# Layer 2 spectra of a four-layer kernel: three samples' image norms stepped behind the stages of the next sample's 7x7 windows, and two samples' transforms interleaved

## The chip, the cores and the metric

The kernel runs on one core of a Trainium2 chip. The metric is the device time of one execution in microseconds. All data and arithmetic of the parts discussed here are float32.

## The reference, cut to what matters

The input is `x`, (4, 56, 56, 128). Four layers follow each other, each with a group norm in front and a residual around it: a 7x7 window attention with a global attention and an MLP (layer 0), an edge network (layer 1), a Fourier-operator attention over images (layer 2), and a temporal convolution (layer 3). Only the entry of layer 2 is touched.

```python
x = x + _L2_conv_ref(_gn(x), ...)          # _gn: group norm, 32 groups of 4 channels
# inside layer 2; B, T, H, W = 4, 56, 56, 128 (a 56 x 128 image per row of the tensor)
xa = x.reshape(B * T, 1, H, W)
xa_n = _inorm(xa, norm_g[0], norm_b[0])    # mean and variance of each whole image
k = _fno_layer(xa_n, wK, wKs, bKs, (H // 2, W // 2))   # each begins with rfft2(xa_n)
q = _fno_layer(xa_n, wQ, wQs, bQs, (H // 2, W // 2))
v = _fno_layer(xa_n, wV, wVs, bVs, (H, W))
```

So before any spectrum can be formed, a sample needs its group norm (mean and variance of 4 channels over all pixels) and its 56 image norms (mean and variance of 56 x 128 values each). The kernel calls the group-normed sample `xad`. It needs it again later, as the residual of layer 2.

## The kernel before, in words

A sample lies in SBUF as 128 partitions (channels) by 3136 pixels. Layers 0 and 1 run sample by sample, in `first_layers`: `fast_windows` (7x7 window attention, layer norm and the projections for the global attention), the rest of `fast_attention` (global attention), `mlp`, `edge_layer`. Their result is the tile `x1`, which is stored to DRAM as `x2d[b]` (L2424). A value that is computed at run time chooses between this fast path and a general one (`tc.If`); the fast path is the one that runs, and behind the branch all engines go on in the code for layers 2 and 3.

`fast_windows` takes a sample's 64 windows in 8 groups of 8. It is a software pipeline with 10 stages (norm, project, score, value, turn, output, central, variance, attended, divide), written out in Python loops over `n` and over the stages: at each `n` stage s works on group n minus that stage's lag. The order of TensorE (PE), VectorE (DVE) and ScalarE (ACT) is exactly the order of the Python code (`manual_schedule`). Three PSUM banks tagged `mm` rotate among the stages. After groups 3 and 7, `variance` takes a square root on ACT (L434) and a reciprocal of 128x392 on DVE (L435), which `divide` needs. Matrix products for global attention start only when the last group has left the pipeline.

Layer 2 begins in `spectra`, once all four samples are done. `normed_images` makes a sample's norms: 56 `bn_stats` (L1209), an aggregate (L1213), two small products on PE with `g4` for the group mean and variance (L1215, L1231), a square root (L1233), the scaling of the whole sample in place (`apply_norm`, L192), the store to `xad` (L1237), and two more small products for the image means and variances (L1243, L1249) with a square root and a reciprocal. `sample_spectra` makes a sample's transforms: 224 small products over the image width (L1271), scaled into `z` by DVE (L1273) and copied by ACT (L1275), then the products over the height (L1281, L1293 with ACT copies, and L1303 with copies shared by DVE and ACT). Both are generators. The last sample is still in SBUF (`x1`) and goes first: all its norms, then its transforms; the norms of the next sample are stepped between the pieces of the transforms, and whatever is left of them runs before the next transform begins. The other three samples are loaded back from `x2d` (L1203).

SyncE (SP) issues nearly all DMAs, in an order which the framework's scheduler chooses and which then is fixed. GpSimd (POOL) prepares the weights of the spectral layers (`all_score_weights`, `value_weights`) at the same time as the spectra.

Of the kernel before, what the change touches and what calls it, by code (L numbers as in the profile page):

```python
# [18 lines left out]
P = 128  # L19
# [279 lines left out]

def both_attentions(k, w, xw, xf):  # L300
    window_attention(k, w, xw, xf)
    global_attention(k, w, xf)


def fast_windows(k, w, xw, xf, mr, Q, K, V):

# [15 lines left out]
    with ExitStack() as es:  # L322
# [103 lines left out]
        def variance(g):  # L426
            q = g % HALF
            if q == 0:
                roots[g // HALF] = psum.tile([P, 512], F32, tag="var", name="w_var", bufs=1)
            var = roots[g // HALF]  # L430
            nc.tensor.matmul(var[32 * q:32 * q + 32, :N], k.ones_c[:, 0:32], squares.pop(g), start=True, stop=True)
            if q == HALF - 1:
                r = wk.tile([P, N], F32, name="w_r")
                nc.scalar.activation(r, var[:, :N], AF.Sqrt, scale=1024.0, bias=eps)  # L434
                nc.vector.reciprocal(r, r)  # L435
                roots[g // HALF] = r
# [9 lines left out]
        def attended(g):  # L446
# [7 lines left out]
            while chunk < 25 and (g == NG - 1 or chunk * P + 4 * P <= b.stop):  # L454
# [8 lines left out]
                chunk += m  # L463

        norm(0)
        norm(1)
        for n in range(NG + 11):
            for stage, g in ((norm, n + 2), (project, n), (score, n - 1), (value, n - 2), (turn, n - 3), (output, n - 4),
                             (central, n - 5), (variance, n - 6), (attended, n - 11), (divide, n - 10)):
                if 0 <= g < NG:  # L470
                    stage(g)


# [85 lines left out]

def fast_attention(k, w, xw, xf, mr):  # L560

# [8 lines left out]
    with ExitStack() as es:  # L570
# [3 lines left out]
        va = big.tile([P, 25, P], F32, name="f_va")  # L574
        fast_windows(k, w, xw, xf, mr, qT, kT, va)

# [610 lines left out]

def normed_images(k, w, st, b, pools, x2d, xad, ready):

    nc = k.nc
    wk, psum = pools

    def tiny(name):
        return wk.tile([P, HH], F32, name="s_" + name)

    if st.last == b:
        xp = st.x1
    else:  # L1200
        xp = wk.tile([P, HH + 1, HH], F32, name="s_x2")
        for t in range(0, HH, 28):
            nc.sync.dma_start(xp[:, t:t + 28, :], x2d[b, :, t:t + 28, :])  # L1203
        yield
    nc.vector.memset(xp[:, HH, :], 0.0)
    x = xp[:, :HH, :]
    rows = wk.tile([P, HH, 6], F32, name="s_rows")
    for t in range(HH):
        nc.vector.bn_stats(rows[:, t, :], x[:, t, :])  # L1209
        if t % 8 == 7:  # L1210
            yield
    mv = wk.tile([P, 2], F32, name="s_mv")
    nc.vector.bn_aggr(mv, rows.rearrange("p a b -> p (a b)"))  # L1213
    ps = psum.tile([P, 512], F32, tag="t", name="s_pt")
    nc.tensor.matmul(ps[:, 0:1], k.g4, mv[:, 0:1], start=True, stop=True)  # L1215

    half = [rows[:, :, i] for i in range(6)]
    mean, sq, d = tiny("mean"), tiny("sq"), tiny("d")
    nc.vector.tensor_sub(d, half[1], half[4])
    nc.vector.tensor_mul(d, d, d)  # L1220
    nc.vector.tensor_add(sq, half[2], half[5])
    nc.vector.scalar_tensor_tensor(sq, d, HH / 4, sq, ALU.mult, ALU.add)
    nc.vector.tensor_add(mean, half[1], half[4])
    yield
    mr = wk.tile([P, 2], F32, name="s_mr")
    t1 = wk.tile([P, 1], F32, name="s_t1")
    nc.vector.tensor_copy(mr[:, 0:1], ps[:, 0:1])
    nc.vector.tensor_sub(t1, mv[:, 0:1], mr[:, 0:1])
    nc.vector.tensor_mul(t1, t1, t1)
    nc.vector.tensor_add(t1, t1, mv[:, 1:2])  # L1230
    nc.tensor.matmul(ps[:, 1:2], k.g4, t1, start=True, stop=True)  # L1231
    yield
    nc.scalar.activation(t1, ps[:, 1:2], AF.Sqrt, bias=k.eps)  # L1233
    yield
    nc.vector.reciprocal(mr[:, 1:2], t1)
    apply_norm(k, x, x, mr)
    nc.sync.dma_start(xad[b], x)  # L1237
    ready[b] = xp
    yield
    nc.vector.tensor_scalar(mean, mean, 0.5, mr[:, 0:1], ALU.mult, ALU.subtract)  # L1240
    nc.vector.tensor_scalar_mul(mean, mean, mr[:, 1:2])
    nc.vector.tensor_scalar(sq, sq, mr[:, 1:2], mr[:, 1:2], ALU.mult, ALU.mult)
    nc.tensor.matmul(ps[:, 64:64 + HH], k.ones_c, mean, start=True, stop=True)  # L1243
    yield
    nc.vector.tensor_copy(st.norm[:, b, 0, :], ps[:, 64:64 + HH])
    nc.vector.tensor_sub(d, mean, st.norm[:, b, 0, :])
    nc.vector.tensor_mul(d, d, d)
    nc.vector.scalar_tensor_tensor(sq, d, float(HH), sq, ALU.mult, ALU.add)
    nc.tensor.matmul(ps[:, 128:128 + HH], k.ones_px, sq, start=True, stop=True)  # L1249
    yield  # L1250
    nc.scalar.activation(d, ps[:, 128:128 + HH], AF.Sqrt, bias=k.eps)
    yield
    nc.vector.reciprocal(d, d)
    nc.vector.tensor_scalar_mul(st.norm[:, b, 1, :], d, w.ng[:, 0:1])
    yield


def sample_spectra(k, st, b, pools, x):

    nc = k.nc
    wk, psum = pools

    z = wk.tile([P, 33, 2 * HH], F32, name="s_z")
    xf = x.rearrange("p t h -> p (t h)")
    for t0 in range(0, HH, 14):
        ps = psum.tile([P, 512], F32, tag="row", name="s_pr")
        for t in range(14):
            for ri in range(2):  # L1270
                nc.tensor.matmul(ps[64 * ri:64 * ri + 64, t * 33:(t + 1) * 33],  # L1271
                                 xf[:, (t0 + t) * HH:(t0 + t) * HH + 64], k.fw[:, ri, :], start=True, stop=True)
        nc.vector.tensor_mul(z[:, :, t0:t0 + 14], ps[:, :462].rearrange("p (t f) -> p f t", t=14),  # L1273
                             bc(st.norm[:, b, 1, t0:t0 + 14], 1, 33))
        nc.scalar.copy(z[:, :, HH + t0:HH + t0 + 14], z[:, :, t0:t0 + 14])  # L1275
        yield
    o = slice(64 * (b % 2), 64 * (b % 2) + 64)
    for c0, c1, v in C_BLOCKS_S:
        ps = psum.tile([P, 512], F32, tag="acc", name="s_ps")
        m = (c1 - c0) * HH  # L1280
# [8 lines left out]
    for blocks in (C_BLOCKS_R[:2], C_BLOCKS_R[2:]):  # L1289
        ps = psum.tile([P, 512], F32, tag="acc", name="s_pr2")  # L1290
        for i, (c0, c1, v) in enumerate(blocks):
# [8 lines left out]
    for c0 in range(0, 32, 4):  # L1300
        ps = psum.tile([P, 512], F32, tag="acc", name="s_px")
        for i in range(4):
# [5 lines left out]

def spectra(k, w, st, x2d, xad):

# [3 lines left out]
    for t in (st.S, st.iS, st.R):  # L1314
        nc.gpsimd.memset(t[:, :, :, HH:], 0.0)
    ready = {}
    with ExitStack() as es:
# [4 lines left out]
                                                     mybir.EngineType.DVE}))  # L1322

        order = [st.last] + [b for b in range(B) if b != st.last]
        norms = [normed_images(k, w, st, b, (wk, tiny), x2d, xad, ready) for b in order] + [iter(())]
        next(norms[1])
        for _ in norms[0]:
            pass
        for n, b in enumerate(order):
            ahead = norms[n + 1]  # L1330
            for _ in sample_spectra(k, st, b, (wk, psum), ready.pop(b)):
                next(ahead, None)
            for _ in ahead:
                pass

# [1032 lines left out]
def build(k, packs, I, out):  # L2368
# [3 lines left out]
    with ExitStack() as es:  # L2372
# [10 lines left out]

        l2p = es.enter_context(tc.tile_pool(name="l2", bufs=1))
        with tc.tile_pool(name="w01", bufs=1) as wp, tc.tile_pool(name="io", bufs=1) as io:
            xw = io.tile([P, TOK], F32, name="xw")
# [29 lines left out]
            def first_layers(attention, x, to, loaded=False):  # L2416
# [6 lines left out]
                edge_layer(k, w1, x1, st)  # L2423
                nc.sync.dma_start(to, x1)  # L2424

            with tc.If(small_scores > 0) as small:
                for b in range(B):
                    first_layers(lambda *a: fast_attention(*a, k.mr[:, b, :]), I["x"][b], x2d[b],
                                 loaded=b == 0)
            with small.Else():  # L2430
                with tc.For_i(0, B, 1) as b:
                    first_layers(both_attentions, I["x"][bass.ds(b, 1)].rearrange("b p t -> (b p) t"),
                                 x2d[bass.ds(b, 1)].rearrange("b p l n -> (b p) l n"))

        l3p = es.enter_context(tc.tile_pool(name="l3", bufs=1))
        load_weights(k, l3p, I, "w3_", w2)
        load_weights(k, l3p, I, "w2_", w2, only=CONV_WEIGHTS)
        st = Env()
        st.x1, st.last = x1w, B - 1
        st.norm = l3p.tile([P, B, 2, HH], F32, name="norm")  # L2440
        st.AbT = l3p.tile([P, 2, HH], F32, name="AbT")
        st.dc = l3p.tile([1, B, HH], F32, name="dc")
        with tc.tile_pool(name="xh", bufs=1) as xp:
            st.xh = xp.tile([112, B, 2, 32, HH], F32, name="xh")
            with tc.tile_pool(name="sp", bufs=1) as sp:
# [4 lines left out]
                with tc.tile_pool(name="g_wk", bufs=1, side="right") as wk:  # L2450
                    all_score_weights(k, I, w2, sp, wk, st)
                    value_weights(k, I, w2, wk, dd)
                    spectra(k, w2, st, x2d, xad)
                x1s.close()
# [32 lines left out]
```

## Time and profile before

| | us |
|---|---|
| median of 3 runs (lowest to highest) | 3901.99 (3901.64 to 3906.46) |
| profiled execution, its own time | 3907.5 |
| its span, first to last instruction | 3905.7 |
| `fast_windows` of samples 0, 1, 2, 3, to the first product of the global attention | 53.8 to 155.5, 759.9 to 860.1, 1463.4 to 1563.1, 2168.7 to 2269.0 |
| last instruction of the last edge layer (DVE L966) | 2869.2 to 2869.9 |
| spectra: first `bn_stats` (L1209) to last copy into `xh` (ACT L229) | 2872.2 to 2913.0 for the first of the four samples, to 3013.4 for all |

The mean granted TensorE clock of the execution is 0.954. Of the span PE is busy 91%, DVE 74%, ACT 53%, POOL 30%.

Times in the profile are microseconds from the start of the span, unless ns is written. A line number is that of the kernel before. A row of a timeline or of the chain has start, duration, engine, line, operation or tile, and a count; square brackets hold the idle time of the engine before the row and what ended it. A table of windows has, for each stretch, its length and the busy time and instruction count of PE, PEld (weight loads), DVE, ACT and POOL, then the granted clock and the DMA share and rate.

### The profile page before, as it was taken

To read this page: it belongs to the slowest core of one execution; us is meant where nothing else is said; L and a number is where in the kernel's file an instruction comes from. 1 tells how busy PE (TensorE), PEld (TensorE's weight loads), DVE (VectorE), ACT (ScalarE), POOL (GpSimd) and SP (SyncE) were. 2 spreads that over 40 slices of the span, in tenths; PEclk is the share of its full clock that TensorE was granted. 3 is DMA by queue.
4 is the path that set the end of the run, shared out by engine and by line. 5 is a ranking of instruction groups with operands and counts; after the bars stand their busy time and mean duration, and the time that the engine had idled before them with its cause. 6 is when DMAs were issued, how large, how long until landed. Compare 5 with 4: busy or idle time off the path is not lost. (4 is left out here: it accounts for less than half of the span.)

```text
span 3905.7 us, 79417 instructions
## 1 busy us (share of the span) xinstructions
PE 3553.4 (91%) x35416; PEld 1604.1 (41%) x35416; DVE 2891.3 (74%) x2759; ACT 2086.9 (53%) x2108; POOL 1156.6 (30%) x563
## 2 busy tenths in 40 slices
PE   6899989989998899999889999998967989989988
PEld 4432234542323455232245532224446433336564
DVE  6588877758887785888779578886965767775654
ACT  4577765457776544877655467774622012215332
POOL 0000006600000470000027100001851769984656
PEclk8999999999999999999999999999978999999888
DMA  2000000000000000000000000000031048841101
GB/s 95 1 1 1 1 17 2 19 1 1 1 1 1 18 3 18 1 1 1 1 18 3 18 1 1 1 1 1 3 112 61 1 98 177 165 111 70 52 7 50
DMA packets 73497, 111.13 MB, mean 28 GB/s; under 512 B 62140, under 2 KB 63932, under 8 KB 67900
## 3 DMA queue, kind: packets, MB, share of 16 engines
q1 hardware_dynamic: 14460, 93.13, 8.0%
q10 hardware_dynamic: 58688, 12.85, 2.0%
q8 instruction: 280, 4.59, 0.5%
q14 instruction: 69, 0.57, 0.1%
HBM read 79.46 MB, written 26.51 MB: 27 GB/s over the span
## 5 line engine op out<-in xcount | busy, mean ns | idle before, releaser
L651 ACT ACTIVATE f_ring<-f_s 128x1792 f32<-128x1792 f32 (+3 forms) x796 | 1097.7, 1429 | 231.5 <-PE f_s L649 229.6
L594 DVE TENSOR_TENSOR f_acc<-f_acc,f_ring 128x1792 f32<-128x1792 f32 x560 | 1134.0, 2025 | 66.1 <-ACT f_ring L651 9.3
L988 POOL TENSOR_TENSOR e_tp<-e_a,e_c 128x1792 f32<-128x1792 f32 x140 | 451.7, 3259 | 2288.1 <-ACT e_a L951 2183.7
L649 PE MATMUL f_s<-f_qT,f_kT 32*128 32x448 f32 x5376 | 741.4, 574 | 47.8 <-ACT f_ring L651 27.1
L600 PE MATMUL f_po<-f_ring,f_va 128*32 128x448 f32 x5376 | 592.0, 548 | 0.0
L986 DVE TENSOR_TENSOR e_td<-e_pa,e_c 128x1792 f32<-128x1792 f32 x252 | 491.4, 2015 | 14.4 <-ACT e_a L951 14.4
L649 PEld LDWEIGHTS f_s<-f_qT,f_kT 32*128 32x128 f32 x5376 | 269.7, 184 | 526.4 <-ACT f_ring L651 382.5
L993 PE MATMUL e_acc<-e_td,t_shared 32*32 32x448 f32 x8064 | 322.2, 545 | 20.9 <-DVE e_td L986 10.0
L990 ACT ACTIVATE e_tp<-e_tp 128x1792 f32<-128x1792 f32 x140 | 235.1, 1697 | 173.2 <-POOL e_tp L988 173.1
L1589 DVE TENSOR_TENSOR u_ud<-u_px,u_d 112x1792 f32<-112x1792 f32 x144 | 240.1, 1708 | 94.8 <-PE u_po L1594 85.7
L600 PEld LDWEIGHTS f_po<-f_ring,f_va 128*32 128x32 f32 x5376 | 133.5, 109 | 398.0 <-issue 397.0
L993 PE MATMUL e_acc<-e_tp,t_shared 32*32 32x448 f32 x4480 | 220.5, 544 | 3.1 <-ACT e_tp L990 2.5
L1594 PE MATMUL u_po<-u_ud,AT 112*64 112x448 f32 x960 | 200.7, 548 | 23.3 <-DVE u_ud L1589 23.3
L1591 POOL TENSOR_TENSOR u_up<-xh,u_d 112x1792 f32<-112x1792 f32 x64 | 193.8, 3054 | 24.1 <-PE u_po L1594 12.4
L993 PEld LDWEIGHTS e_acc<-e_td,t_shared 32*32 32x32 f32 x8064 | 133.8, 103 | 145.7 <-DVE e_td L986 56.0
L617 DVE RECIPROCAL f_den<-f_den 128x448 f32<-128x448 f32 x28 | 82.7, 2953 | 77.5 <-ACT f_den L616 77.5
L1594 PE MATMUL u_po<-u_up,AT 112*64 112x448 f32 x576 | 125.2, 541 | 0.9 <-POOL u_up L1591 0.9
L1594 PEld LDWEIGHTS u_po<-u_ud,AT 112*64 112x64 f32 x960 | 64.9, 137 | 147.6 <-issue 86.5
L594 DVE TENSOR_TENSOR f_acc<-f_ring 128x1792 f32<-128x1792 f32 x28 | 56.7, 2025 | 90.0 <-ACT f_ring L651 60.3
L865 ACT ACTIVATE m_hT<-m_ph,w_fb 128x392 f32<-128x392 f32 x128 | 72.7, 588 | 83.7 <-PE m_ph L864 78.2
L993 PEld LDWEIGHTS e_acc<-e_tp,t_shared 32*32 32x32 f32 x4480 | 94.4, 103 | 55.3 <-ACT e_tp L990 19.4
L1456 POOL TENSOR_TENSOR q_u<-iS,q_g 128x1792 f32<-128x1792 f32 x32 | 102.8, 3236 | 23.9 <-PE q_acc L1471 23.9
(467 smaller groups left out, 4710.2 us busy)
## 6 DMA issues: line engine op xcount, KB each, us to landing
u_d<-dd SPq DMA_DIRECT2D x48, 784.0 KB
xw<-in_x SPq DMA_DIRECT2D x4, 1568.0 KB
x2d<-x SPq DMA_DIRECT2D x4, 1568.0 KB
x_xs<-xad ACTq DMA_DIRECT2D x32, 196.0 KB
xm<-x_ev ACTq DMA_DIRECT2D x64, 98.0 KB
o_a<-xm SPq DMA_DIRECT2D x8, 784.0 KB
o_x<-x2d SPq DMA_DIRECT2D x4, 1568.0 KB
out<-o_o SPq DMA_DIRECT2D x12, 448.0 KB
```

Source lines behind the costliest of these rows:

```text
L594: nc.vector.tensor_add(acc, slots(j, 0) if c == 1 else acc, slots(j, c))
L600: nc.tensor.matmul(po[heads[h], :NB], va[o, c, heads[h]], p, start=(c == 0), stop=(c == 24))
L649: nc.tensor.matmul(ss[:, i, :NB], kT[heads[h], c * P:(c + 1) * P], qT[heads[h], blk(j)], start=True, stop=True)
L651: nc.scalar.activation(ring[:, slot:slot + m, :], ss[:, :m, :NB], AF.Exp, scale=scale)
L986: nc.vector.tensor_tensor(t, am, cm, ALU.max)
L988: nc.gpsimd.tensor_sub(t, bc(a.rearrange("p (l n) -> p l n", l=8), 1, 4), cm)
L990: nc.scalar.activation(tf, tf, AF.Relu)
L993: nc.tensor.matmul(acc[quarters[q], r, :NB], k.ident[o, o], t[o, q].rearrange("p l n -> p (l n)"), start=(g == 0), stop=(g == len(EDGE_TUR ...
L1456: nc.gpsimd.tensor_mul(u, bc(st.iS[:, bp, c, :HH], 1, HEADS), bc(g[:, n, c, :], 2, HH))
L1589: nc.vector.tensor_mul(u, bc(px[:, :, :NB], 2, m), dm)
L1591: nc.gpsimd.tensor_mul(u, bc(x, 2, m), dm)
L1594: nc.tensor.matmul(po[64 * b2:64 * b2 + 64, :NB], st.AT[:, 8 * i + h0 + q, 2 * bp + b2, :], u[:, b2, q, :], start=(left == 16), stop=(left ...
```

## The change

1. `normed_images` is cut into 50 small steps (two `bn_stats` to a step, one product to a step, the scaling in quarters). Its products each get a bank of their own from the caller, and a result that ACT read from PSUM before is copied out by DVE first. Just ahead of each of its two square roots it yields the word "root".
2. `fast_windows` of samples 1, 2 and 3 calls one such step, for the sample before, after every stage call. After "root" it makes no step until the stage `variance` has taken its own square root; then the next step, which holds the norm's square root, comes right there.
3. So `x1` of samples 0, 1 and 2 is normed in place during the following sample's windows and stored to `xad`. `x2d` is still stored for the first three in the branch; that of the last sample is stored behind it.
4. Behind the branch, the group-normed samples 0 and 1 are loaded from `xad` into a pool of two tiles next to `x1`, sample 2 into the first of them when it is free.
5. `spectra` takes samples in the order 0, 1, 2, 3. The products over the width are a generator of their own (`first_transform`) with four pieces per sample. Sample 0's run first; those of sample b+1 go behind pieces 2, 5, 7 and 9 of the 13 pieces of sample b's remaining transforms. The norm of sample 3 is stepped beside them, three steps to a piece.
6. The PSUM tag `acc` of the spectra has four banks where it had three.

The core of the diff:

```diff
 def fast_windows(k, w, xw, xf, mr, beside, Q, K, V):
...
                 nc.scalar.activation(r, var[:, :N], AF.Sqrt, scale=1024.0, bias=eps)
+                step(True)
                 nc.vector.reciprocal(r, r)
...
+        steps = beside(bank)
+        root_next = False
+
+        def step(root):
+            nonlocal root_next
+            if root or not root_next:
+                root_next = next(steps, None) == "root"
...
                 if 0 <= g < NG:
                     stage(g)
+                    step(False)
...
-def normed_images(k, w, st, b, pools, x2d, xad, ready):
+def normed_images(k, w, st, b, wk, bank, xp, xad):
...
     for t in range(HH):
         nc.vector.bn_stats(rows[:, t, :], x[:, t, :])
-        if t % 8 == 7:
+        if t % 2 == 1:
             yield
...
+    yield
+    ps = bank()
     nc.tensor.matmul(ps[:, 0:1], k.g4, mv[:, 0:1], start=True, stop=True)
+    yield
...
+    yield "root"
+    nc.scalar.activation(t1, var, AF.Sqrt, bias=k.eps)
     yield
...
+    for t in range(0, HH, 14):
+        apply_norm(k, x[:, t:t + 14, :], x[:, t:t + 14, :], mr)
+        if t == 42:
+            nc.sync.dma_start(xad, x)
+        yield "root" if t == 42 else None
+    nc.scalar.activation(d, d, AF.Sqrt, bias=k.eps)
...
-def spectra(k, w, st, x2d, xad):
+def spectra(k, w, st, xad, images):
...
+        norm = normed_images(k, w, st, B - 1, wk, lambda: tiny.tile(...), st.x1, xad[B - 1])
+        zs = {}
+        first = [first_transform(k, st, b, (wk, psum), st.x1 if b == B - 1 else images(b), zs) for b in range(B)]
+        for _ in first[0]:
             pass
...
+        for b in range(B):
+            for n, _ in enumerate(sample_spectra(k, st, b, (wk, psum), zs.pop(b))):
+                for _ in range(3):
+                    next(norm, None)
+                if b < B - 1 and n in (2, 5, 7, 9):
+                    next(first[b + 1])
...
+        def images(b):
+            if b not in loaded:
+                xp = loaded[b] = x2p.tile([P, HH + 1, HH], F32, name="s_x2")
+                for t in range(0, HH, 28):
+                    nc.sync.dma_start(xp[:, t:t + 28, :], xad[b, :, t:t + 28, :])
+                nc.gpsimd.memset(xp[:, HH, :], 0.0)
+            return loaded[b]
+
+        loaded = {}
+        for b in range(2):
+            images(b)
+        nc.sync.dma_start(x2d[B - 1], x1)
```

## The prediction

> **What bounds the kernel now.** I read the page first, for the share of each engine over the span, then the chain of waits around the spectra, then tables of windows for the two places that the change joins, then timelines of single engines there. The page says that PE rules the whole, and is short of work in few slices; slices 30 and 31 of 40 (2831 to 3027) are two of them.
>
> ```profile
> span 3905.7 us, 79417 instructions
> ...
> PE   6899989989998899999889999998967989989988
> ...
> POOL 0000006600000470000027100001851769984656
> ```
>
> The chain of waits from the last edge layer to the attention weights shows the spectra as a row of alternations: DVE statistics, a product, DVE again, then PE.
>
> ```profile
> 2869.26 2.82 issue
> 2872.17 6.65 DVE s_rows L1209 x56
> ...
> 2890.77 12.12 PE s_pr L1271 x224
> ...
> 2928.51 6.68 PE s_pr L1271 x224
> 2935.21 0.64 DVE s_z L1273
> 2935.85 4.73 DVE s_rows L1209 x40
> ...
> 2994.66 7.16 PE s_pr L1271 x224
> ...
> 3007.09 5.77 PE s_px L1303 x56
> ```
>
> The windows tell how full PE is. The rows are sample 1's windows with a stretch from their middle, the end of sample 3's, then the spectra: norms of the first sample, a whole middle sample, and the transforms of the last, which has no norm beside it.
>
> ```profile
> 759.90:860.10 100.20, 89.14 (x726) 55.51 (x726) 53.87 (x102) 47.70 (x80) 8.76 (x22) 0.95 0.04 17
> 780.00:800.00 20.00, 20.00 (x273) 15.69 (x270) 13.50 (x33) 13.56 (x24) 0.00 (x0) 1.00 0.01 2
> 2226.00:2269.00 43.00, 35.63 (x128) 17.63 (x126) 16.88 (x24) 15.46 (x27) 0.00 (x0) 0.96 0.00 0
> 2872.00:2891.00 19.00, 2.69 (x14) 2.30 (x16) 16.63 (x93) 0.45 (x2) 8.37 (x20) 0.52 0.83 286
> 2928.50:2961.00 32.50, 23.47 (x310) 20.98 (x309) 18.82 (x86) 8.45 (x19) 0.00 (x0) 0.75 0.32 126
> 2994.70:3013.00 18.30, 16.76 (x300) 14.79 (x300) 5.05 (x8) 8.18 (x18) 0.00 (x0) 0.97 0.02 4
> ```
>
> A middle sample takes 32.5 us, the last 18.3 us: the difference is the norm. From 2872 to 2891 PE has 2.7 us of work in 19. In the windows PE is full in the middle and DVE is busy 54% of the stage.
>
> **Removed from the spectra.** Three terms.
>
> Ahead of the first product: now PE ends its last edge product at 2869.1 and begins L1271 at 2890.8, behind the last sample's whole norm. After the change it needs only sample 0's normed image. SP's own order in the trace runs ahead (it loads `xw` for the next sample at 579.9, in the middle of the MLP). The last thing that SP has in the branch is then `xad[2]` near 2235 and no longer `x2d<-x` at 2869.90. The two new tiles lie beside `x1`, which only the tiles of the global attention reach down to, and that ends near 2650. So I take both images as there before 2869, and PE begins at about 2869.6. DVE comes out of the branch at 2872.1 either way. The other end: SP is held to the end of the branch; samples 0 and 1 then travel ahead of the weights. The row to price it: `s_x`, 1.5 MB, issued at 2881.39, in use by 2894.55 when DVE gets to it; that is at most 13 us, I say 12 later.
>
> The 224 products at 2890.77 take 12.12 us, those at 2928.51 take 6.68; the granted clock is 0.50 in the first stretch and 1.00 in the second. Begun 0.5 us after the edge products (clock 0.97 from 2869 to 2873) they should cost 6.7. The Trainium skill, "TensorE: Matmul & The Clock Gate", Part 1, says that an idle window of about 3.4 us halves the clock and a busy one restores it; by it a start 5 us late would begin at half clock for about 3.4 us and lose some 1.7 us (an estimate), not the 5.4 us that these rows differ by. The trace is on the side of a longer cold spell.
>
> Per sample: PE needs 16.76 - 7.16 + 6.7 = 16.3 us for one sample at full clock (last row above, first product at the middle sample's price). With `first_transform` of sample b+1 between the pieces of sample b this work is continuous for samples 0 to 2.
>
> New end of the spectra: 2869.6 + 6.7 + 0.7 (last L1273, 0.64) = 2877.0; three samples at 16.3 are 48.9; the last one has no next transform beside it and costs what it costs now from its last L1273 (3001.84) to its last copy (3013.4), 11.6. That is 2937.5. To this I add what the norm of sample 3 does beside samples 0 and 1. It has 4 products, each behind a DVE step in front of it: bn aggregate 1.67, three small ones 0.5 with 0.6 for the product before, and so on, about 1.2 each, 5 in all. And DVE ops suffer from POOL, which prepares weights from 2877 to 2918: L1222 took 2.95 there against 0.22 in a sample without POOL, and the scaling 2.83 against 1.91.
>
> ```profile
> 2909.69 2.95 DVE L1222 SCALAR_TENSOR_TENSOR s_sq<-s_d,s_sq 128x56 f32<-128x56 f32 x1
> 2916.81 2.83 DVE L192 TENSOR_SCALAR s_x<-s_x,s_mr 128x3136 f32<-128x3136 f32 x1
> ...
> 2942.83 0.22 DVE L1222 SCALAR_TENSOR_TENSOR s_sq<-s_d,s_sq 128x56 f32<-128x56 f32 x1
> ```
>
> These two lost 3.6 us; before, three such ops at 2887 to 2890 lost 2 more. I add 3, with 0 and 12 as ends (about ten POOL ops of 1.2 met in turn). Here a rule speaks against the change: the Trainium skill, "SBUF - State Buffer", SBUF: two separate sides, says that VectorE with two SBUF inputs or in its faster modes, and GpSimd, exclude each other for a whole instruction. By it every such step of the norm can wait for a POOL op, and the sum would use the 12. The rows show single ops hit and most not, so I keep 3.
>
> End: 2937.5 + 5 + 3 = 2945.5 against 3013.4. Gain 68. Bounds: 76 with none of the additions, 47 with 12 for POOL and 12 for late images at once. What follows is not late: POOL ends its weights near 2918, the DMAs to and from `apart` keep their distance to the last sample, and image 2 (free to load when PE leaves sample 0's first transform, 2876.3) lands 11 to 13 us after its issue near 2881, before its first use near 2877 + 16.3 + 4 = 2897.
>
> **Added to three window stages.** The same steps run in the windows of samples 1, 2, 3. Samples 1, 2, 3 have 100 us there now. There are 51 stage calls before group 3's `variance` and the first "root" is after step 35, so all steps find room and the square roots fall where the table is loaded already.
>
> - 28 pairs of `bn_stats`: 56 in 6.65 us. During the first six n DVE has about 4.3 us of work in a 6.5 us turn while PE is full (20.0 of 20). Seven pairs are 1.7 to 2.2 us a turn: it just fits. I take 1.5 on the path, from 0 to 6.65.
> - Four small products on PE, of which each takes two passes (L1215 x2 0.38, L1243 x2 0.65): 0.4 each, 1.6, straight on PE's path.
> - PE waits behind them. The first stands behind the aggregate: PE would reach it at the end of `value`, DVE ends the last `vd` copy plus a pair plus 1.67 about 1.1 us later. The second waits for three small ops, 0.7. The third is the bad one: it stands after `output(6)`, and its input comes after DVE's reciprocal. In the timelines of DVE and PE of sample 3:
>
> ```profile
> 2229.66 2.60 DVE L435 RECIPROCAL w_r<-w_r 128x392 f32<-128x392 f32 x1 [1.58 <-ACT w_r L434]
> ...
> 2232.94 0.92 PE L443 MATMUL w_mm<-w_r,c_ones 32*128 32x392 f32 x2 [2.42 <-ACT w_oT L229]
> ```
>
> PE does `central(5)` and `variance(4)` (2228.75 to 2230.5) before that idle time. With the product ahead of them they move behind the reciprocal and three small ops: 1.6 + 0.7 = 2.3. The fourth, behind `divide(0)`, waits for four small ops: 0.8. Sum 4.9.
> - Scaling in quarters, 1.91 in all, and the last small ops, in the tail, where DVE is busy 16.88 of 43: 1.0 of 1.91 plus 0.3.
>
> Sum 1.5 + 1.6 + 4.9 + 1.3 = 9.3 a stage, 28 for three. Low end 4 a stage (products 1.6, third wait 2.3), high end 18: all DVE work at full price, 6.65 + 1.67 + 1.91 + about 1.5, with the 1.6 and 4.9. The store of `xad` comes under the global attention, with DMA at 0.00 to 0.01; x1 is written next in the MLP 450 us later: nothing.
>
> Sum: -68 + 28 = -40. Against the profiled execution's own 3907.5 that is 3867.5; against the median 3902.0 it is 3862. A difference under 0.2% (7.8 us) is about what a measurement of this kernel cannot tell from none.
>
> **Rivals.** (1) The branch holds SP: the images arrive 12 us late and PE starts cold, 3874. For it speaks that the loads stand behind the branch in the kernel; against it that SP's loads run ahead elsewhere. (2) Image 2 is queued behind `dd<-d_f`, which SP issues at 2918.0 when POOL is done: PE has no work for about 22 us at sample 1, 3884. Before, `s_x` of the next sample was in fact issued only at 2920.1, behind that DMA. Against it: the load is free to go at 2876, long before `dd`. (3) Slower: each PE wait in the windows is not absorbed but moves the whole pipeline, the bank that a norm's product holds until DVE's copy stalls the rotation of three, and the clock falls with it (0.91 granted in 820 to 840 already). The decisive point is 68 / 3 = 23 us a stage; at 26, the sum of all DVE work 11.7, products 1.6, and doubled waits 9.8, with 3 for the banks, it is 78 against 68: 3912. Against it: DVE is idle for 46% of the stage. (4) The steps run but the gain isn't there since POOL's weights end last: POOL would need to end after 2945, 27 us later than now; weights are issued from 2871.3 now and would start as early, so I give it little.
>
> **How the numbers follow.** Forecast 0.74, (1) 0.10, (2) 0.08, (3) 0.05, (4) 0.03. The range: low end 76 gained for 12 paid, 3838; high end 47 gained for 36 paid (12 a stage) is 3891, and it takes in (1) and (2). Of the forecast and these two, about a tenth lies outside. Faster by over 0.2%: 0.90, from the forecast, (1), (2); within: 0.04, from (4) and the edges; slower 0.06, (3) and what I can't see.
>
> **What would show it.** Right: L1271 begins within 1 us of the branch's end and takes about 6.7 for the first sample; last copy into `xh` near 2945 + 28 = 2973 in the new span; clock near 1.0 in the spectra; no L1209 before L1271 on the chain; windows of samples 1 to 3 at 105 to 112 us and sample 0's still 101.7. Wrong: PE idle at its first or third transform behind a DMA, or windows over 120 us.

## The result, and the profile after

The changed kernel takes 3893.84 us (median of 4 runs, 3887.05 to 3900.11) against 3901.81 us for the kernel before beside it; the ratio is 0.9978, interval 0.9959 to 0.9998. Timed once more (e11, 12 runs) it was 3897.99 us, ratio 0.9982, 0.9970 to 0.9994. So it is faster, by 6 to 8 us and not by the 40 forecast, and 3893.84 lies above the top of the range, 3891. The gain is 0.2%, about what the prediction called the limit of what can be told from none; both intervals end below 1, the first only just. The profiled execution takes 3892.77 us against 3907.5.

The page still says 91% for PE. Its two weak slices around the spectra, 6 and 7 before, read 9 and 8 now.

```profile
span 3891.0 us, 79411 instructions
...
PE   6899989989998898999989989998998989989988
```

Two tables of windows settle the accounts. First of before: the windows of sample 2 and the whole spectra, from the last edge operation to the last copy into `xh`. Then of after: the windows of samples 1, 2, 3 and the same stretch of the spectra. Columns as before: length, busy PE, PEld, DVE, ACT, POOL, granted clock, DMA share, GB/s.

```profile
1464.10:1563.10 99.00, 88.45 (x724) 54.96 (x724) 53.47 (x101) 47.70 (x80) 8.47 (x19) 0.97 0.04 17
2869.90:3013.40 143.50, 95.98 (x1232) 85.47 (x1232) 82.91 (x361) 34.11 (x76) 35.41 (x57) 0.71 0.31 114
```

```profile
751.70:864.60 112.90, 96.20 (x732) 57.79 (x732) 68.06 (x182) 48.12 (x82) 8.13 (x19) 0.91 0.07 29
1465.10:1578.00 112.90, 96.20 (x732) 57.82 (x732) 68.04 (x182) 48.12 (x82) 8.12 (x19) 0.91 0.07 30
2182.30:2291.00 108.70, 91.98 (x732) 56.47 (x733) 67.95 (x182) 48.13 (x82) 8.12 (x19) 0.95 0.07 31
2897.70:2995.30 97.60, 77.87 (x1208) 67.59 (x1208) 48.80 (x132) 32.06 (x70) 34.98 (x58) 0.83 0.26 89
```

The spectra give 143.5 - 97.6 = 45.9 (forecast 68). The windows, 298.2 before from the last edge operation to the first score product, are 334.7: they take 36.5 (forecast 28). That leaves 9.4. The other 5 us between the two profiled executions lie in parts whose code is the same; the start up to sample 0's last edge operation alone differs by 8.9.

The chain of waits through the spectra of after (start, length, engine, tile, line, count):

```profile
2897.92 5.11 PE s_pr L1291 x168
2903.02 1.95 issue
2904.97 0.65 DVE s_z L1293
...
2905.66 3.14 PE s_pr L1291 x56
...
2923.21 2.71 DVE t_w_M L1719
...
2926.70 6.99 DVE t_w_M L1720
2933.69 3.53 DVE t_w_M L1722
...
2937.30 0.59 PE s_pt L1219 x2
...
2968.93 1.65 PE s_ps L1307 x6
...
2988.15 6.57 PE s_px L1329 x64
```

PE does begin 0.2 us behind the last edge operation (2897.7). Two things then stand in its way, and the waits name them (engine, line, what it waited for, total, times, longest):

```profile
PE s_pt L1219 <- DVE s_mv L1216: 13.7, 1, 13.7
...
DVE s_z L1293 <- issue: 7.3, 1, 7.3
```

DVE comes to its first `s_z` only at 2904.97, so PE runs out of banks after three quarters of the transform (the tag of `s_pr` has three, with 56 products to a bank). And PE waits 13.7 us for the norm's aggregate, which stands on DVE behind small operations of `conv_weights`. Those ran at 2878.9 to 2881.8 before, 0.15 to 0.19 us each; now they lie in the middle of POOL's weights. From the timelines of DVE and POOL:

```profile
2926.62 7.07 DVE L1720 TENSOR_TENSOR t_w_M<-t_w_M,t_w_M0rev 112x1 f32<-112x1 f32 x1
2933.61 3.61 DVE L1722 TENSOR_SCALAR t_w_M<-t_w_M 112x62 f32<-112x62 f32 x1
```

```profile
2931.74 1.12 POOL L1381 TENSOR_TENSOR d_t<-t_w_P,t_w_V 128x448 f32<-128x448 f32 x1
2932.82 0.24 POOL L1414 TENSOR_TENSOR q_t<-t_w_qk 128x32 f32<-128x32 f32 x1
2933.05 1.39 POOL L1385 TENSOR_SCALAR d_t<-t_w_V,t_images 128x448 f32<-128x448 f32 x1
...
2935.73 0.35 POOL L1427 TENSOR_SCALAR q_g<-q_g,t_images 128x32 f32<-128x32 f32 x1
2936.05 1.12 POOL L1386 TENSOR_TENSOR d_d<-d_d,d_t 128x448 f32<-128x448 f32 x1
2937.27 1.70 POOL L1385 TENSOR_SCALAR d_t<-t_w_V,t_images 128x448 f32<-128x448 f32 x1
```

L1720 adds one column and takes 7.07 us, while POOL runs from one TENSOR_TENSOR into the next (each begins 0.02 to 0.04 us before the last one ends). It ends 0.64 us into a TENSOR_SCALAR of POOL (L1385). Not every TENSOR_SCALAR lets an operation through: L1722, which follows, outlasts L1427 and ends at 2937.22, in the gap of 0.10 us behind L1386.

### The profile page after: what moved, and what is told of

Its sections match the earlier page's. It is cut to its first block, busy times and chain, and to the rows that moved or that the text cites. A ratio compares the mean times of both kernels' runs of the same rounds, so it can differ in the third digit from the quotient of the medians.

```text
span 3891.0 us, 79411 instructions
## 1 busy us (share of the span) xinstructions
PE 3545.8 (91%) x35416; PEld 1587.4 (41%) x35416; DVE 2900.7 (75%) x2771; ACT 2084.2 (54%) x2108; POOL 1156.5 (30%) x567
## 5 line engine op out<-in xcount | busy, mean ns | idle before, releaser
L1614 DVE TENSOR_TENSOR u_ud<-u_px,u_d 112x1792 f32<-112x1792 f32 x144 | 240.1, 1708 | 94.8 <-PE u_po L1619 83.7
L1616 POOL TENSOR_TENSOR u_up<-xh,u_d 112x1792 f32<-112x1792 f32 x64 | 193.8, 3057 | 24.0 <-PE u_po L1619 12.4
```

Source lines behind the costliest of these rows:

```text
L1614: nc.vector.tensor_mul(u, bc(px[:, :, :NB], 2, m), dm)
L1616: nc.gpsimd.tensor_mul(u, bc(x, 2, m), dm)
```

## The experiments

Stage lengths inside one trace say more here than times: the windows of after, in seven traces that share their code, add up to 332.8 to 334.7 us, while the times of one kernel lie up to 24 us apart. Stage lengths are not free of scatter either: e6 and e9 share the code of their windows and differ by 9.6 us there, and e11, which is the changed kernel once more, has spectra of 101.0 us where after has 97.6. Each stage length is from one trace. The tables give them for the runs that bear on each stretch. Spectra are cut at the first `s_ps` product (L1307) of each sample; "entry" is the first transform of sample 0.

| spectra, us | whole | entry | sample 0 | 1 | 2 | 3 |
|---|---|---|---|---|---|---|
| forecast | 75.6 | 7.4 | 16.3, and 8 for the norm | 16.3 | 16.3 | 11.6 |
| after | 97.6 | 11.6 | 38.2 | 21.0 | 16.6 | 9.9 |
| e1_conv_late | 93.3 | 7.5 | 36.9 | 22.1 | 16.6 | 9.9 |
| e2_store_late | 90.6 | 10.8 | 35.2 | 17.9 | 16.6 | 9.9 |
| e4_no_pool | 87.1 | 12.6, begun 2.1 late | 26.4 | 19.5 | 16.6 | 9.9 |
| e5_norm_from_1 | 83.2 | 7.5 | 17.7 | 31.1 | 16.8 | 9.9 |
| e8_one_by_one | 107.4 | 13.0 | 47.5 | 19.8 | 16.9 | 10.0 |
| e10_skip_4 | 81.5 | 7.5 | 17.5 | 28.2 | 18.2 | 9.9 |
| e11_after_again | 101.0 | 12.0 | 40.1 | 22.2 | 16.6 | 9.9 |

| windows of samples 1, 2, 3, us | length | PE idle | granted clock |
|---|---|---|---|
| before | 99.5, 99.1, 99.6 | 10.3, 10.6, 11.3 | 0.95, 0.97, 0.97 |
| after | 113.0, 113.0, 108.7 | 16.8, 16.8, 16.8 | 0.91, 0.91, 0.95 |
| e3_root_later | 108.0, 109.6, 108.7 | 16.0, 16.0, 15.3 | 0.95, 0.94, 0.94 |
| e6_spread | 107.6, 107.6, 109.0 | 17.0, 17.0, 16.7 | 0.97, 0.97, 0.95 |
| e7_no_products | 111.2, 104.4, 105.8 | 12.4, 13.7, 13.8 | 0.86, 0.95, 0.94 |
| e9_both | 107.5, 117.4, 109.0 | 16.9, 16.1, 16.7 | 0.97, 0.87, 0.95 |
| e10_skip_4 | 107.2, 108.0, 105.5 | 13.1, 13.2, 14.7 | 0.94, 0.92, 0.97 |
| e11_after_again | 111.8, 113.0, 108.7 | 15.2, 16.8, 16.8 | 0.89, 0.91, 0.95 |

**e1_conv_late**: is it these operations, or the place? Cut to what matters; the call behind the attention, where they stood, keeps only a tile that is needed later.

```
             if b < B - 1 and n in (2, 5, 7, 9):
                 next(first[b + 1])
+            if b == B - 1 and n == 0:
+                conv_weights(k, w, pool)
```

> Edit: the 22 DVE ops that prepare the weights of the last layers (M0, M1, W and their factors) are made in the DVE order behind the first piece of sample 3's transforms, when POOL has ended its own weights; everything else is as in the changed kernel. There the stretch from the last edge op to the last copy into xh is 97.6 us, with 13.7 us of PE waiting for the aggregate. Theory A (those ops, with two SBUF inputs or a fast mode, are shut out by POOL's run of work and hold the norm behind them): the wait falls under 3 us, the stretch to 85 to 88, the whole by about 10. Theory B (whatever stands there is shut out, so the norm's own small ops take over the wait): the stretch stays at 94 to 98. Theory C (the wait has nothing to do with POOL): unchanged, 97 to 98.

The place. PE waits 10.4 us, now for L1225 of the norm: with `conv_weights` gone, the norm's own small operations are held. Samples 0 and 1 together take 59.1 us against 59.2. From the timelines of DVE and of POOL in this run:

```profile
2924.44 0.15 DVE L1223 COPY s_mr<-s_pt 128x1 f32<-128x1 f32 x1
2924.63 3.60 DVE L1224 TENSOR_TENSOR s_t<-s_mv,s_mr 128x1 f32<-128x1 f32 x1
2928.26 7.74 DVE L1225 SCALAR_TENSOR_TENSOR s_t<-s_t,s_mv 128x1 f32<-128x1 f32 x1
```

```profile
2928.19 0.36 POOL L1406 TENSOR_SCALAR q_skip<-t_images 128x32 f32<-128x32 f32 x1
...
2934.04 1.12 POOL L1383 TENSOR_TENSOR d_t<-t_w_P,t_w_V 128x448 f32<-128x448 f32 x1
2935.13 0.24 POOL L1416 TENSOR_TENSOR q_t<-t_w_qk 128x32 f32<-128x32 f32 x1
2935.36 1.39 POOL L1387 TENSOR_SCALAR d_t<-t_w_V,t_images 128x448 f32<-128x448 f32 x1
```

L1224 ends at 2928.23, 0.04 us after L1406 begins; L1225 ends at 2936.0, 0.6 us into L1387. The copy out of PSUM (L1223) took its usual 0.15. That the stretch is nevertheless 4.3 us shorter, and so just under theory B's 94 to 98, comes from the entry, 7.5 us for 11.6: DVE's first `s_z` follows the edge by 2.5 us there and by 7.3 in after. The time is 3891.9 us, ratio 0.9967 (0.9954 to 0.9980).

**e4_no_pool** takes POOL's arithmetic on the score and value weights away; these are then zero.

> Edit: POOL's arithmetic on the score and value weights is left out (they are set to zero; their DMAs stay), the rest is as in the changed kernel. Theories A and B: no DVE op in the spectra takes more than twice its time elsewhere, PE never waits 13.7 us, and the stretch from the last edge op to the last copy into xh falls from 97.6 to 80 to 84. Theory C: 95 to 98.

```profile
2906.05 5.98 PE s_pr L1291 x106
...
2928.00 1.59 DVE s_mv L1216
...
2929.64 0.38 PE s_pt L1219 x2
...
2941.01 2.81 PE s_ps L1307 x4
```

What stands ahead of the norm's first product in this chain is DVE's own work: 1.59 us for the aggregate, 1 us of small operations, and two of `conv_weights` with 0.06 and 0.07. Samples 0 and 1 take 45.8 us against 59.2: by these two traces POOL's price is 13.4 us (16.5 against e11's 62.3). The whole stretch, 87.1, misses the 80 to 84 mostly by its entry, 2.9 us longer than in after: PE began 2.1 us late and DVE 8.5 us behind the branch.

**e2_store_late** asks what holds DVE at the entry.

```
-        nc.sync.dma_start(x2d[B - 1], x1)
...
                 spectra(k, w2, st, xad, images)
+                nc.sync.dma_start(x2d[B - 1], x1)
```

> Edit: the store of the last sample's x2d is issued behind the spectra instead of at their head (it then stores the normed sample, so the residual of sample 3 is wrong). In the changed kernel DVE does its last edge op at 2897.0 and its first scaling L1293 at 2905.0, though its first inputs were there at 2899. Theory F1 (DVE's code is loaded behind the 1.6 MB of that store): DVE's first L1293 comes about 3 us after the last edge op, as in the kernel before, and the first transform costs 7 us and not 12. Theory F2 (the store has no part in it): still 7 to 8 us after.

DVE's first `s_z` still comes 6.8 us behind the edge, near F2's 7 to 8, so it is not the store's traffic. The trace's DMA records tell more: packets of queue 14, whose kind is instruction, start at 2898.05 and 2903.20 in after, and DVE's next instructions start 1.84 us (a semaphore) and 1.77 us (L1293) behind these. That the packets carry DVE's code is read from such times. In e2 the second comes at 2902.34, L1293 at 2904.36; in e4 at 2904.70 and 2906.51. In e1 it comes at 2904.19 and DVE waits 0.31 us at 2905.9, behind the fourth `s_z`: there the first block held all four. So the times point to the place where a block of DVE's code ends after the branch; no run changes that place alone. The run's stretch is 7 us shorter all the same: without the store the weights landed earlier, and most of `conv_weights` was through by 2914.1, held for 1.2 us at most. Three operations that came later (L1732 to L1734) took 1.1, 3.5 and 3.6 us, and PE's wait was 10.1.

**e5_norm_from_1** moves the norm of sample 3 (with e1's edit).

```
-                for _ in range(3):
+                for _ in range(4 * (b > 0)):
                     next(norm, None)
```

> conv_weights is late as in e1, and the norm of sample 3 takes its steps from b == 1 on, four a piece, so it stands behind POOL's run of weights (which ended at 2945 in e1) and no longer in it. Theory B (whatever stands in POOL's run is shut out): the 10.4 us that PE waited for L1225 in e1 go and nothing of DVE is longer than alone (L1224 0.16, L1225 0.22); from the last edge op to the last copy into xh 79 to 84 us, against 93.2 in e1 and 97.6 after. Rival: the norm is now too late, and PE waits for it at the first transform of sample 3 or at one of its four products: 86 to 94.

83.2 us, as theory B said, but not quite for the reason that it gave: POOL's run ended at 2948.9 and the norm's small steps begin at 2939.8, within its tail. L1224 and L1225 took 0.16 and 0.22 us under a TENSOR_SCALAR of POOL:

```profile
2939.40 1.39 POOL L1387 TENSOR_SCALAR d_t<-t_w_V,t_images 128x448 f32<-128x448 f32 x1
```

```profile
2939.94 0.16 DVE L1224 TENSOR_TENSOR s_t<-s_mv,s_mr 128x1 f32<-128x1 f32 x1
2940.14 0.22 DVE L1225 SCALAR_TENSOR_TENSOR s_t<-s_t,s_mv 128x1 f32<-128x1 f32 x1
```

L1238, L1240 and L1241, later, each waited out one TENSOR_TENSOR (1.13 to 1.22 us). The time is 3881.9 us, ratio 0.9932 (0.9914 to 0.9950).

**e8_one_by_one** undoes the interleave alone.

```
-                if b < B - 1 and n in (2, 5, 7, 9):
-                    next(first[b + 1])
+            if b < B - 1:
+                for _ in first[b + 1]:
+                    pass
```

> The interleave alone is undone: the first transform of sample b + 1 comes whole behind the last piece of sample b. Theory I1: the interleave covers the turns from PE to DVE and ACT and back; without it each of three samples has PE idle some 1.5 to 3 us more (16.8 busy of 18.3 for the last sample of before), and the spectra stretch is 102 to 107 us against 97.6. Rival I2: the stretch is set by DVE's ops that POOL's run shuts out, so what is lost is taken from PE's 13.7 us at the norm's first product: 96 to 100.

107.4 us, in the range of I1, but I1's mechanism is wrong. Sample 2, which has no norm beside it, takes 16.9 us one by one and 16.6 interleaved: the turns from PE to DVE cost 0.3. The loss is 8.0 us in samples 0 and 1 and 1.4 at the entry. PE still waits 15.0 us for `s_mv`, and the transform that filled part of the norm's waits now comes behind them, at a granted clock of 0.50 all through; the one after it has 1.00:

```profile
2949.53 12.12 PE s_pr L1291 x224
...
2974.79 6.68 PE s_pr L1291 x224
```

So the interleave is worth 6 to 10 us (107.4 against 101.0 in e11 and 97.6 in after), mostly as filler for the norm.

**e3_root_later**: the windows' third product. In after's timeline of PE, its first and third norm products in the windows of sample 2, and the ten microseconds behind the third:

```profile
1507.89 0.35 PE L1219 MATMUL w_mm<-s_mv,t_shared 128*128 128x1 f32 x2 [1.51 <-DVE w_rec L399]
...
1534.98 0.68 PE L1252 MATMUL w_mm<-s_mean,c_ones_c 128*128 128x56 f32 x2 [4.12 <-DVE s_mean L1248]
```

```profile
1535.10:1545.10 10.00, 10.00 (x18) 3.76 (x19) 3.70 (x11) 1.58 (x3) 0.00 (x0) 0.56 0.00 1
```

```
     nc.scalar.activation(t1, var, AF.Sqrt, bias=k.eps)
     yield
     yield
+    yield
+    yield
+    yield
     nc.vector.reciprocal(mr[:, 1:2], t1)
```

> Edit: three empty steps behind the norm's first square root, so that its third product comes behind the first product of divide and no longer ahead of central(5). Windows of samples 1, 2, 3 take 112.9, 112.9 and 108.7 us in the changed kernel and 99.5, 99.0, 99.6 before. Theory W1 (the excess is mostly PE waiting at that product behind DVE's long reciprocal, and the slow clock after it): 107 to 109 each, and no granted clock of 0.56 in a 10 us stretch. Theory W2 (DVE has too much to do, the place of the product does not matter): within 1.5 us of now. The whole falls by 12 to 16 under W1, 0 to 4 under W2.

The windows add up to 326.4, 8.3 less: nearer to W1, but one stage is over its 109, and the whole is 3 to 7 us below after and not 12 to 16. The 4.12 us turn back into the 2.42 that stood there before, and at most 0.6 ahead of the product, and no stretch of ten microseconds has 0.56. But idle time fell by 0.8 to 1.4 us a stage only. The rest is the clock: PE's busy time, for the same work, went from 96.2 to 92.1 and 93.7 in the first two stages, and from 92.0 to 93.4 in the third. Nor does the wait fix the clock: in after the ten microseconds behind the same 4.12 have 0.57, 0.56 and 0.84 in the three stages. 3890.9 us, ratio 0.9960 (0.9940 to 0.9980).

**e6_spread** adds room ahead of the first two products (two empty steps behind the aggregate, one behind L1225).

> The windows of e3 (root later) and besides two empty steps between the aggregate and the first product, one between L1225 and the second. Theory W1: PE's idle time of 1.5 us ahead of the first product and of 0.3 ahead of the second goes, the rest stays: windows of samples 1, 2, 3 at 106 to 108 us each (108.1, 109.6, 108.7 in e3), some 5 less in sum; a half-clock spell more or less moves one of them by 1 to 4. Rival W2: DVE's own work sets the windows, and the idle time turns up at the next product: 108 to 110 each, no change in sum.

A half miss: 324.3 in sum, 2.1 less than e3. The idle time did not go (17.0, 17.0, 16.7, for 16.0, 16.0, 15.3 in e3): 1.33 us of it now stands ahead of `central`'s product (L423) instead of the norm's, as W2 had it. What fell is PE's busy time, by 5.5 us in sum, at a higher clock. 3888.8 us, ratio 0.9958 (0.9941 to 0.9975).

**e7_no_products** leaves the products out.

> The norms in the windows of samples 1, 2, 3 leave out their four products and the banks for them; DVE takes the input of each product in place of its result (so those norms are not the reference's); all DVE, ACT and DMA steps stay. Theory W1 (products and the waits ahead of them are most of the price): windows of 102 to 105 us each, against 99.3 without norms and 112.9, 112.9, 108.7 with them: what stays is idle time behind bn_stats at the start (1.05 to 2.8), the scaling and the steps in the tail, some 3 to 5. Rival W2 (DVE's 15 us of added work are the price): 107 to 110.

Idle time falls to 12.4, 13.7, 13.8 us: the products, with their banks, account for some 3.5 of the 6.0 us added a stage, DVE's steps for the rest. One stage is in W1's range (104.4), one just above it (105.8); the first is 111.2 with less idle time than any other stage with norms, at clock 0.86. What made it longer than the second was the clock alone: PE is busy 98.8 us there and 90.6 in the second.

**e9_both** joins e5 and e6.

> The windows of e6 (three products moved away from the DVE steps that feed them) and the spectra of e5 (conv_weights late, norm of sample 3 behind POOL's run) in one kernel. If the two are independent, as the stages' spans say, windows 322 to 328 us in sum (324.2 in e6) and spectra 81 to 86 (83.2 in e5; the norm has three to six more empty steps), together 30 to 38 less than the 441.7 of before: ratio 0.990 to 0.993. Rival: the three to six more steps bring the norm's last products so late that PE waits for the first transform of sample 3: spectra 88 to 95, ratio 0.992 to 0.995.

The spectra are 81.4, as expected. The windows are 333.9, beyond the 322 to 328: the second is 117.4, where e6, with the same instructions and an idle time of 17.0, took 107.6. The rows are the second stage of e6, then of e9:

```profile
1468.00:1575.60 107.60, 90.67 (x732) 55.63 (x732) 67.73 (x182) 47.95 (x82) 8.16 (x19) 0.97 0.07 31
```

```profile
1462.80:1580.10 117.30, 101.26 (x732) 59.95 (x733) 67.73 (x182) 48.00 (x82) 8.12 (x19) 0.87 0.07 28
...
1532.80:1542.80 10.00, 9.38 (x16) 3.88 (x16) 2.60 (x10) 2.26 (x4) 0.00 (x0) 0.50 0.00 1
```

3882.0 us, ratio 0.9941 (0.9928 to 0.9953): short of the 0.990 to 0.993 expected.

**e10_skip_4** is e9 with the norm's steps in the windows begun four stage calls later.

```
-        steps = beside(bank)
+        steps = itertools.chain((None,) * 4, beside(bank))
```

> As e9, and the norm's steps in the windows begin four stage calls later, so no bn_stats pair stands ahead of DVE's first inputs to PE. If the 2.8 us of idle time at 3.9 us of a window stage (1.05 to 2.56 before) come from these pairs, it falls to 1.0 to 1.7 and windows are 318 to 325 in sum. Rival: that idle time has nothing to do with bn_stats (2.56 once in before, without any), and the sum stays at 322 to 328, give or take a half-clock spell of 4.

3870.86 us (3862.58 to 3877.67), ratio 0.9910 (0.9895 to 0.9926): the best version, 33 us faster than before. Its windows and its spectra:

```profile
757.40:864.60 107.20, 94.08 (x732) 57.25 (x732) 67.02 (x183) 48.08 (x82) 8.21 (x19) 0.94 0.07 31
1470.10:1578.00 107.90, 94.74 (x732) 57.66 (x733) 66.97 (x182) 48.08 (x82) 8.14 (x19) 0.92 0.08 31
2185.30:2290.80 105.50, 90.75 (x732) 55.81 (x733) 66.94 (x183) 48.06 (x82) 8.23 (x19) 0.97 0.08 32
2893.60:2975.10 81.50, 75.27 (x1208) 66.27 (x1208) 39.55 (x138) 32.03 (x70) 35.02 (x58) 0.90 0.31 106
```

The windows are 320.7, in the range, though the idle time early in the stage is 0.9, 1.6 and 2.6 us: in one stage it stayed, so `bn_stats` is not its only cause. What else went are the idle times ahead of the norm's second product (0.75 to 0.92 us in e9, now 0.14 to 0.16) and of `central`'s (1.33, now 0.30). Of the 13.2 us less than in e9's windows 8.5 are idle time and 4.7 the clock. The times of the two, taken beside each other, differ by 11 us, and their intervals do not overlap. Against after, windows 14 and spectra 16 us less; the times differ by 27.

**e11_after_again**, the changed kernel beside these two:

> The changed kernel once more, timed beside the two above. Ratio to before 0.996 to 0.9985, as it was (0.9978); the same three stages: windows 331 to 336 in sum, spectra 95 to 99.

333.5 and 101.0 us, the latter beyond its 95 to 99; the ratio as before.

## Why the prediction was wrong

The sign, the start and the order of events held; two terms of the sum were mis-sized. The range ended at 47 gained for 36 paid. Both terms came out past that corner, 45.9 and 36.5; the sum's own high end for the windows, 18 a stage, was not taken into the range.

**The spectra term, 45.9 for 68.** Four parts make up nearly all of the 22 us:

- POOL against DVE: 3 was added, 13.4 it was (e4), beyond even the upper end of 12. This is the step that failed. The prediction argued that most rows were not hit, and even its upper end met POOL's operations one at a time. That most were not hit was true of before's order, in which `conv_weights` and the first norm ran ahead of POOL's dense run. The change moves the code, and with it which small operations meet that run. And an operation that meets it can be held for several of POOL's, as the prediction's own row of L1222, 2909.69 to 2912.64, already was. POOL's operations beside it in before:

```profile
2910.03 1.11 POOL L1357 TENSOR_TENSOR d_d<-d_d,d_t 128x448 f32<-128x448 f32 x1
2911.13 0.35 POOL L1402 TENSOR_SCALAR q_g<-q_g,t_images 128x32 f32<-128x32 f32 x1
2911.45 1.11 POOL L1361 TENSOR_TENSOR d_d<-d_d,d_t 128x448 f32<-128x448 f32 x1
2912.66 1.43 POOL L1360 TENSOR_SCALAR d_t<-t_w_V,t_images 128x448 f32<-128x448 f32 x1
```

It ended in the gap of 0.1 us behind the second TENSOR_TENSOR. The rule weighed there (the Trainium skill, "SBUF — State Buffer", SBUF: two separate sides) pointed the right way and was set aside. Its "for the whole instruction" is too mild for the 7.07 and 7.74 us, each of which ran across ten or more of POOL's.
- The norm's four products beside the transforms: 5 was added. In e4, without POOL's arithmetic, samples 0 and 1 take 45.8 us against 32.6 for the work alone: by subtraction 13.2. PE waits at each product for a DVE chain, and runs at half clock behind it (56 `s_pr` products in 3.13 us where 1.75 is usual).
- The entry, 11.6 for 7.4: PE was early, as forecast, but the prediction let DVE follow 2.9 us behind the branch as before ("DVE comes out of the branch at 2872.1 either way") and priced no second block of its code. With DVE there in time, in e1, it is 7.5.
- The last sample, 9.9 for 11.6, gave 1.7 back.

**The windows term, 36.5 for 28.** Its idle part was too high, not too low: 4.9 of waits and 2.8 for DVE's steps, against 6.0 us of added idle time a stage (16.77 for 10.74). The third wait added 4.12 - 2.42 = 1.7 for 2.3. What failed is the term that is not in the sum: the clock. PE's busy time grew by 6.1 us a stage (94.8 against 88.7 in the mean), of which the four products took 2.1 (1.6 in the sum); the other 4.0 are the same matmuls at a granted clock of 0.91, 0.91, 0.95 in place of 0.95 to 0.97. The prediction put a lower clock only into its rival (3).

**Rivals.** (1) and (2) fell: L1291 starts with the images there, and no transform waits for one. (3) was right in its kind, waits with a lower clock, but at 12.2 us a stage, half its decisive 23. (4) did not happen as written: POOL ended at 2942.9, long before the spectra. But POOL was on the path all the same, by holding DVE.

**The signs listed.** L1291 within 1 us: yes (0.2). No statistics ahead of the first product on the chain: yes. First transform 6.7: no, held by DVE, where the list thought of DMA only. Last copy near 2973: 2995.3. Clock near 1.0: 0.83. Windows 105 to 112: two at 113.0, one at 108.7; sample 0's, without norms, 98.9. Neither sign of being wrong came up: no transform waited for a DMA, and no windows took over 120.

What decides in which windows the clock falls was not settled.

## What to carry to other kernels

When a change moves work, list for each moved DVE operation what POOL is doing at that moment, in the new order and not the old: two small DVE operations under POOL's run cost PE 10 us (e1), and with the norm moved by one sample as well (e5) the gain on before was 25 us, where e1 had 12 and the change alone 6 to 8. A product that is fed by DVE step by step wants other PE work between the step and itself, enough to cover the step (in e6 such room only moved the idle time to another product; in e10 it went); without it the price is the wait and the slower clock behind it. Price the clock in any stage where PE's idle time grows, even when each wait looks small.

## What the runs showed of the hardware

- DVE's operations whose tensors all lie in SBUF (TENSOR_TENSOR, TENSOR_SCALAR, SCALAR_TENSOR_TENSOR) were held for up to 9.87 us (L1725 of e6; 7.07 in after, 7.74 in e1) through rows of POOL operations, nearly all TENSOR_TENSORs of 0.24 to 1.26 us each. The longest holds ended under a POOL TENSOR_SCALAR of 0.36 or 1.39 us, others in a gap of about 0.1 us. But the 9.87 us ran past a TENSOR_SCALAR of 0.36 us (L1410), the one of `q_g` by `t_images` (0.35 us; L1427 of after and e2, L1429 of e1, L1402 of before) ended no hold, and several operations came through between two TENSOR_TENSORs (L1733 and L1225 of e2, L1255 of e1, L1240 of e5). Which one comes through when is not settled. Under a TENSOR_SCALAR two of these operations took 0.16 and 0.22 us (e5). Those reading PSUM (L1293, 0.64; L1223, 0.15) and `bn_stats` (0.20) kept their price under POOL's run, and so did the aggregate in e1 and e5 (1.67); in after it took 3.51, between two held operations.
- The same instructions with nearly the same waits took 107.6 and 117.4 us in a window stage, with granted clocks of 0.97 and 0.87. The Trainium skill, "TensorE: Matmul & The Clock Gate", Part 1, says that the activity window of about 3.4 us runs freely and that the number of cold matmuls differs from run to run. These two rows agree that it differs, by 10 us; that the window's phase is the reason no run here shows. Nor did a full PE always bring the clock back: the transform at 2949.53 in e8 ran all its 12.12 us at 0.50, as the one at 2890.77 in before did, so the 3.4 us that the prediction weighed for that one hold for neither.
- Behind a branch DVE's instructions came 1.8 to 2.0 us after a packet that by its time carries DVE's code, and a second packet, some 4 to 7 us after the first, could hold it again. The same kernel timed again (e11) had an entry of 12.0 us for 11.6, and three empty steps in another stage (e3) one of 13.6.
